# Queries and keys of a cosine attention, transposed by VectorE blocks and DMA through DRAM instead of by TensorE

## The chip, the cores and the metric

The kernel runs on one core of a Trainium2 chip. The metric is device time in microseconds (us) for one execution. The kernel is one program for a model of four layers. TensorE multiplies, and can transpose by multiplying with an identity matrix. VectorE, ScalarE and GpSimd work element by element or reduce along a row. SyncE issues the DMAs that concern us. Each engine works through its own list of instructions in the order in which the build put them, and waits where an input is not there yet.

## The reference

Input `x` is 2048 tokens of 512 features. Layer 0 is a rotary attention and a gated MLP, layer 2 a latent attention, layer 3 a set of grouped experts. The change is in layer 1, whose attention is a cosine attention. The kernel handles it as 8 batches of 256 tokens with 16 heads of 32 features; everything is f32:

```python
qkv = (xin @ Wqkv.T + qkv_bias)                  # q, k, v: 16 heads x 32
sm = exp(minimum(scale_mul_log, log(100)))       # one number for each head
qn = q / maximum(norm(q), 1e-12) * sm            # norm over the 32 features of a head
kn = k / maximum(norm(k), 1e-12)
p  = softmax(einsum('bhqd,bhkd->bhqk', qn, kn) + attn_bias)
o  = einsum('bhqk,bhkd->bhqd', p, v)
x  = x + (o @ Wproj.T + bproj) * gamma1
```

A query and a key come out of the projection with tokens on the partitions and features along the row. The scores need them turned, with the 32 features of a head on the partitions. That turn is what is changed.

## The kernel before

**Tiles.** A token tile is 128 tokens by 512 features; a batch is two of them, `t` = 0 and 1 (`TB` = 2). `KC` = 4 is the number of blocks of 128 features. PSUM is used in two rings of four banks: "A" for scores, "C" for all else. The tags `qT` and `kT` have two buffers each, `qk` four.

**The attention loop** (`attend`, line L655 on) has one round for each batch and each group of four heads, so 32 rounds. A round does this, in the program's order:

- `scored` (L697): eight score products for the four heads of the group, into four "A" banks.
- `turned` (L783): transposes by TensorE of the last group's weights of heads 2 and 3, first half.
- `softmax`: on VectorE a first pass (L743) that adds the bias and finds each row's lowest, on ScalarE the exponential (L747), eight of each. Heads 0 and 1 of a group are "in blocks" in all batches but the last: their weights are turned by VectorE in blocks of 32x32 (L752), written to DRAM in four DMAs (`put`, L549), and fetched back with the blocks in place (L756). For that their keys are read in runs of 32 elements. The other two heads' weights are turned by TensorE and copied out of PSUM (L480, L483).
- `some(quantum)`: work out of a queue (below).
- second half of `turned`, then `weighted` (L808: weights times v) and `divided` (L830, a context copy on VectorE that also divides), with `some` between.

**The queue** holds Python generators: the projection of the next batch (`project1`) and the outcome of the one before (`finish`: eight products with `w1o`, L631, then `gated`: a bias add on VectorE, L1454, and two multiplies/adds on GpSimd, L1455 and L1456). A generator yields after a bit of work and says what it took in us; `some` goes on until its credit is used. The credit of a batch is `work` = (22.1, 6.8), so many us for the projection and for the outcome, divided over the rounds. This sets only where in the program the work is written. A scheduler in the build then sets the order on every engine by priorities and its own costs.

**The projection** (`project1`, L1458 to L1535) does q and then k for t = 0 and for t = 1, then v for both. Each is four products of 128x512 (L631, through `part` and `product_steps`). For q VectorE adds the bias (L1495) and ScalarE squares (L1496); for k ScalarE squares (L1498) and copies (L1499). VectorE sums the squares for each head (L1501). GpSimd then takes a maximum with 1e-24 (L1503), the power -1/2 (L1504), for q a multiply with `sm` (L1506), and scales the tile (L1508). In the end `turned` (an inner function of the projection with the same name as that of the loop) turns each of the four tiles: four TensorE transposes into a "C" bank (L1479) and one copy into `qT` or `kT` (L480 on VectorE, L483 on ScalarE). The last eight transposes of a batch stand just ahead of the next batch's first scores.

**The start of the stage.** The projection of batch 0 is given to the MLP of layer 0 (`layer1_begin`), which works it off beside its last products (L1073).

Of the kernel before, what the change touches and what calls it, by code (L numbers as in the profile page):

```python
# [87 lines left out]
)  # L88
ROUND = 1.5 * 2.0**23
PI_BELOW = 3.1415925  # L90


def in_blocks(m):
# [86 lines left out]
class Program:  # L180
# [50 lines left out]
    def setup(self):  # L231
        nc, d = self.nc, self.d
        self.const = self.pool("const")
        self.xp = self.pool("xp")
        self.wqkvp = self.pool("wqkvp")
        self.wop = self.pool("wop")
        self.wbigp = self.pool("wbigp")
        self.work = self.pool("work")
        self.psum = self.pool("psum", psum=True)

        def c(shape, tag, **kw):
            return self.t(shape, tag, pool=self.const, **kw)

        self.condT = c([P, KC, 32], "condT")
        nc.gpsimd.memset(self.condT, 0.0)
        nc.sync.dma_start(
            self.condT[:, :, :B], d["condT"].rearrange("(k p) b -> p k b", p=P)
        )
        self.x = [self.t([P, D], f"x{i}", pool=self.xp) for i in range(NT)]
        self.tw = self.columns("tw1T", 1)  # L250
        for i in range(TB):
            self.load_x(i)
        self.vec = c([P, N_VEC], "vec")
        nc.sync.dma_start(self.vec, d["vec"])
        self.pos = c([P, NT], "pos", dtype=I32)
        nc.sync.dma_start(self.pos, d["posT"])
        self.inv_freq = c([P, 32], "inv_freq")
        nc.sync.dma_start(self.inv_freq, d["inv_freq"].to_broadcast([P, 32]))

        self.ident = c([P, P], "ident")  # L260
        make_identity(nc, self.ident)
        self.neg_half = c([P, 32], "neg_half")
        nc.gpsimd.memset(self.neg_half, -0.5)
        self.inv = [c([P, 32], f"inv{i}") for i in range(2)]
        for t in self.inv:
            nc.gpsimd.memset(t, 0.0)
        self.spread = [
            self.tc.dram_tile([32, P], F32, name=f"spread{i}") for i in range(4)
        ]
        self.n_spread = 0  # L270
        self.turns = [self.tc.dram_tile([P, KC * S], F32, name=f"turn{i}") for i in range(3)]
        self.n_turn = 0
        self.flips = [self.tc.dram_tile([P, 8 * P], F32, name=f"flip{i}") for i in range(4)]
        self.n_flip = 0
        self.half_pi = c([P, 1], "half_pi")
        nc.gpsimd.memset(self.half_pi, math.pi / 2)

        self.mod0 = c([P, 8, B], "mod0")
        self.mod1 = c([P, 16, B], "mod1")
        self.mod2 = c([P, 8, B], "mod2")  # L280
        self.mod3 = c([P, 8, B], "mod3")
        self.scondT = c([P, KC, 32], "scondT")
        nc.scalar.activation(self.scondT, self.condT, AF.Silu)
# [371 lines left out]
    def attend(self, name, n_groups, hd, project, value, finish, work, key_tiles=(2, 2), biased=None,  # L655
# [29 lines left out]
        def scored(b, g):  # L685
            lhs_rhs = [got[b][0](g, j) for j in range(4)]
            s = [self.bank("A") for _ in range(4)]
            rows = P // hd
            for j0 in range(0, 4, rows):
                for q in range(TB):  # L690
                    for j in range(j0, j0 + rows):
                        lhsT, rhs = lhs_rhs[j]
                        keys = rhs(wide[q])
                        if j < self.in_blocks(name, b):

                            keys = keys.rearrange("p (k c i) -> p c k i", c=4, i=32)
                        mm = nc.tensor.matmul(  # L697
                            s[j][:, at[q] : at[q] + wide[q]], lhsT(q), keys,
                            start=True, stop=True,
                        )  # L700

                        if name == "attention2" and j == q == 0:
                            self.tc.keep_in_program_order(mm)
            return s
# [562 lines left out]
    def project0(self, b, got):  # L1267
        nc, w, cos, sin = self.nc, self.w0, self.cos, self.sin
        hT = yield from self.h("attention0", b, quick=True)
        yield None  # L1270
        qT = self.t([P, KC, S], "qT")
        kT, v = self.keys_values(b, ((S,), (TB, 64)))
        turn = []
        for t in range(TB):
            i = TB * b + t
            cs, sn = cos[:, i, :], [s[:, i, :] for s in sin]
            tok = slice(t * P, (t + 1) * P)
            q = self.bank("C")
            yield from self.product_steps(q, lambda k: hT[:, k, tok], lambda k: w[:, k, 0:512])
            qr, qb = self.rope(self.bank("qk"), q, cs, sn, 8, 32)  # L1280
            nc.gpsimd.tensor_tensor(qr, qr, qb, ALU.add)
            kv = self.bank("C")
            yield from self.product_steps(
                kv[:, 0:128], lambda k: hT[:, k, tok], lambda k: w[:, k, 512:640]
            )

            kr = self.t([P, P], "kr", 2)
            ka, kb = self.rope(kr[:, 0:64], kv[:, 0:64], cs, sn, 1, 32)
            nc.vector.tensor_copy(v[:, t, :], kv[:, 64:128])
            nc.gpsimd.tensor_tensor(kr[:, 64:128], ka, kb, ALU.add)  # L1290
            nc.gpsimd.tensor_tensor(ka, ka, kb, ALU.add)
            turn.append((t, qr, kr))
        for t, qr, kr in turn:
            yield None
            self.queries_turned(t, qT, kT, qr, kr, 0.125)
            yield 0.53
        if b == 0:
            self.angles(cos, sin, slice(TB, 2 * TB))

        def scores(g, j):  # L1300
            c, i = divmod(4 * g + j, 2)
            rows = slice(64 * i, 64 * i + 64)
            return (
                lambda q: qT[rows, c, q * P : (q + 1) * P],
                lambda n: kT[rows, 0:n],
            )

        got[b] = (scores, v)
# [47 lines left out]
    def layer0_mlp(self):  # L1356
# [54 lines left out]
        def finish(hh, b, ys):  # L1411
# [6 lines left out]
        self.mlp(  # L1418
            ups, downs, down_sums, lambda i: self.layer0_up(4 + i, 1), load_next, act,
            lambda b: self.h("mlp0", b), finish,  # L1420
            (self.layer1_begin(), 22.1),
        )


# [33 lines left out]
    def project1(self, b, got):  # L1458
# [6 lines left out]
        yield None  # L1465

        def part(t, i):
            m = self.bank("C")
            yield from self.product_steps(
                m,  # L1470
                lambda k: hT[:, k, t * P : (t + 1) * P],
                lambda k: w[:, k, i * D : (i + 1) * D],
            )
            return m

        def turned(t, y, yT, at):
            m = self.bank("C")
            for c in range(KC):
                nc.tensor.transpose(  # L1479
                    m[:, c * P : (c + 1) * P], y[:, c * P : (c + 1) * P], self.ident  # L1480
                )
            self.copy(
                t + at, yT[:, :, t * P : (t + 1) * P], m.rearrange("p (c q) -> p c q", c=KC)
            )

        ready = []
        for t in range(TB):
            ss = self.t([P, 32], "ss", 2)
            both = []
            for i in range(2):  # L1490
                m = yield from part(t, i)
                y = self.bank("qk")
# [11 lines left out]
                nc.gpsimd.tensor_tensor(r, r, self.neg_half[:, 0:16], ALU.pow)  # L1504
                if i == 0:
                    nc.gpsimd.tensor_tensor(r, r, self.sm, ALU.mult)  # L1506
                by = r.unsqueeze(2).to_broadcast([P, 16, 32])
                nc.gpsimd.tensor_tensor(heads(y), heads(y), by, ALU.mult)  # L1508
                both.append(y)
            ready.append(both)  # L1510
        qT = self.t([P, KC, S], "qT")
        kT = self.t([P, KC, S], "kT")
        v = self.t([P, TB, D], "v")
        for t in range(TB):
            vp = yield from part(t, 2)
            nc.scalar.copy(v[:, t, :], vp)
            if t == 0:
                turned(0, ready[0][0], qT, 0)
                yield 0.43
                turned(0, ready[0][1], kT, 1)  # L1520
                yield 0.43
        yield None
        turned(1, ready[1][0], qT, 0)
        yield 0.43
        turned(1, ready[1][1], kT, 1)
        yield 0.43

        def scores(g, j):
            rows = slice(32 * j, 32 * j + 32)
            return (  # L1530
                lambda q: qT[rows, g, q * P : (q + 1) * P],
                lambda n: kT[rows, g, 0:n],
            )

        got[b] = (scores, v)  # L1535
# [1 line left out]
    def layer1_attention(self):  # L1537
# [29 lines left out]
        def value(v, g, j, k):  # L1567
            return v[:, k, (4 * g + j) * 32 : (4 * g + j + 1) * 32]

        self.attend(  # L1570
            "attention1", 4, 32, self.project1, value, finish, (22.1, 6.8),
            biased=(self.bias, self.bias_blocks),
            extra={
                4: (self.sums_of_ups(0, 2), 0.0), 5: (self.sums_of_ups(2, 4), 0.0),
# [91 lines left out]
    def project2(self, b, got):  # L1666
# [29 lines left out]
        def scores(g, j):  # L1696
            rows = slice(32 * j, 32 * j + 32)
            return (
                lambda q: qT[rows, g, q * P : (q + 1) * P],
                lambda n: kT[rows, 0:n],  # L1700
            )

        got[b] = (scores, v)
# [194 lines left out]
```

## Time and profile before

| | us |
|---|---|
| median of 3 runs (lowest, highest) | 2083.54 (2082.57, 2085.18) |
| the profiled execution | 2081.64 |
| its span | 2079.8 |
| mean granted TensorE clock in it | 0.989 of full speed |
| the cosine attention in it, from its first score to about the first work of its MLP | 908 to 1257 |
| busy in the whole span: TensorE, VectorE, ScalarE, GpSimd | 2009.4, 1346.3, 747.8, 315.3 |
| busy in 908 to 1257 (349 us): TensorE, VectorE, ScalarE, GpSimd | 343.0, 237.3, 207.0, 166.5 |

A line of a timeline or chain gives the start and the length in us, then engine, tile and source line. "SPq" is the queue of SyncE, on which the DMAs are issued. A name such as "PE C L1479 x8" is eight TensorE instructions of line 1479 that write a "C" bank. A matmul's own duration overlaps with its neighbours, so that a run of eight is shorter than eight times one. The first scores of the batches 0 to 7 start at 907.9, 956.1, 1000.9, 1044.6, 1088.2, 1131.8, 1175.4 and 1216.4 us.

### The profile page before, as it was taken

The numbers are of one execution on the slowest core, as the hardware profiler recorded it, in microseconds if no ns is written. First come the engines' busy times: TensorE is split into PE (matmuls) and PEld (weight loads), VectorE is DVE, ScalarE is ACT, GpSimd is POOL, SyncE is SP. The second block draws the span as 40 slices with busy tenths as digits, with TensorE's granted clock in tenths as the row PEclk, the third lists the DMA queues.
The fourth block names the chain that finished last, engine by engine and source line by source line (L and its number), as shares of the span: only waits on it lengthen the run. The fifth ranks groups of instructions, "written<-read, shape, count | busy, mean of one in ns | idle before, by whom it ended". The sixth has DMA issues, their size and how long they took to land.

```text
span 2079.8 us, 36181 instructions
## 1 busy us (share of the span) xinstructions
PE 2009.4 (97%) x12794; PEld 1469.7 (71%) x12794; DVE 1346.3 (65%) x4398; ACT 747.8 (36%) x2332; POOL 315.3 (15%) x348
## 2 busy tenths in 40 slices
PE   7899999999999999999999999999999989989998
PEld 4555579999999999954444448999999844445443
DVE  6767766656675555756676666766666788766333
ACT  4333331111111111136665653222222256566543
POOL 1111200000000000054545521000000031101120
PEclk9999999999999999999999999999999999999999
DMA  8543361112130000335455543334211245653001
GB/s 305 166 115 92 104 215 48 65 41 64 62 110 26 17 31 16 97 97 129 131 147 139 146 121 109 94 97 122 88 60 40 66 125 133 165 139 87 8 36 41
DMA packets 221523, 202.60 MB, mean 97 GB/s; under 512 B 83296, under 2 KB 184736, under 8 KB 221344
## 3 DMA queue, kind: packets, MB, share of 16 engines
q1 hardware_dynamic: 221344, 200.30, 33.1%
q8 instruction: 102, 1.67, 0.3%
q14 instruction: 77, 0.63, 0.1%
HBM read 132.31 MB, written 67.93 MB: 96 GB/s over the span
## 4 chain that ended last, share of the span: by engine, by line
PE 79%; DVE 7%; ACT 6%; DMA 3%; POOL 2%; issue 2%; SPq 1%; ACTq 0%; DVEq 0%; POOLq 0%
PE C L1024 29%; PE C L631 19%; PE A L1073 18%; PE A L697 4%; PE C L808 3%; ACT p L747 3%; ACT wbig L747 2%; PE C L783 2%; PE A L1766 1%; PE C L1785 1%; DVE st L449 1%; DVE n L650 1%; POOL ss L1504 1%; ACT p L483 1%; DMA turn<-hT 1%
## 5 line engine op out<-in xcount | busy, mean ns | idle before, releaser
L1024 PE MATMUL C<-hT,wbig 128*128 128x128 f32 x3072 | 416.4, 275 | 0.0
L1024 PEld LDWEIGHTS C<-hT,wbig 128*128 128x128 f32 x3072 | 388.8, 192 | 9.0 <-issue 2.4
L631 PE MATMUL C<-wqkv,hT 128*128 128x512 f32 (+1 forms) x768 | 313.4, 549 | 2.1 <-DVE p L480 0.8
L1073 PE MATMUL A<-wbig,p 128*128 128x256 f32 x1024 | 242.2, 379 | 0.0
L631 PEld LDWEIGHTS C<-wqkv,hT 128*128 128x128 f32 x768 | 132.1, 192 | 122.8 <-issue 107.0
L1073 PEld LDWEIGHTS A<-wbig,p 128*128 128x128 f32 x1024 | 189.7, 190 | 23.1
L1054 DVE TENSOR_TENSOR p<-p,C 128x256 f32<-128x256 f32 x192 | 78.9, 418 | 163.2 <-PE C L1024 161.4
L1044 ACT COPY p<-C 128x128 f32<-128x128 f32 x192 | 51.2, 267 | 370.4 <-PE C L1024 361.9
L1024 PE MATMUL C<-ctxT,wbig 128*128 128x128 f32 x1152 | 160.0, 275 | 0.0
L1024 PE MATMUL C<-qk,wbig 128*128 128x128 f32 x1152 | 160.0, 275 | 0.0
L747 ACT ACTIVATE p<-p,low 128x256 f32<-128x256 f32 x256 | 126.8, 497 | 70.0 <-DVE low L743 57.1
L457 POOL TENSOR_SCALAR r<-mv 128x2 f32<-128x2 f32 (+1 forms) x28 | 7.1, 253 | 946.7 <-DVE mv L450 946.7
L1024 PEld LDWEIGHTS C<-qk,wbig 128*128 128x128 f32 x1152 | 144.1, 192 | 0.0
L1024 PEld LDWEIGHTS C<-ctxT,wbig 128*128 128x128 f32 x1152 | 144.1, 192 | 0.0
L747 ACT ACTIVATE wbig<-wbig,low 128x128 f32<-128x128 f32 (+1 forms) x256 | 113.1, 443 | 77.1 <-DVE low L743 77.1
L1398 ACT ACTIVATE p<-C 128x128 f32<-128x128 f32 x64 | 17.8, 278 | 294.9 <-DVE p L1054 294.9
L1045 DVE TENSOR_TENSOR p<-p,C 128x128 f32<-128x128 f32 x192 | 54.6, 284 | 97.7 <-ACT p L1044 97.2
L631 PE MATMUL C<-wo,ctxT 128*128 128x512 f32 x224 | 103.1, 600 | 1.4 <-DVE ctxT L830 1.4
L1504 POOL TENSOR_TENSOR ss<-ss,neg_half 128x16 f32<-128x16 f32 x32 | 93.6, 2925 | 2.7
L747 ACT ACTIVATE p<-A,low 128x256 f32<-128x256 f32 x128 | 59.3, 485 | 87.8 <-DVE low L727 75.8
L697 PE MATMUL A<-kT,qT 32*128 32x256 f32 (+2 forms) x896 | 86.3, 399 | 0.7 <-DVE kT L480 0.4
L743 DVE CUSTOM_DVE_ANT_0 wbig<-A,row 128x128 f32<-128x128 f32 (+1 forms) x256 | 74.0, 351 | 13.5 <-PE A L697 13.4
(244 smaller groups left out, 3431.6 us busy)
## 6 DMA issues: line engine op xcount, KB each, us to landing
flip<-p SPq DMA_DIRECT2D x160, 128.0 KB
p<-flip SPq DMA_DIRECT2D x40, 512.0 KB
turn<-hT SPq DMA_DIRECT2D x120, 128.0 KB
flip<-wbig SPq DMA_DIRECT2D x112, 96.0 KB
wbig<-flip SPq DMA_DIRECT2D x28, 384.0 KB
hT<-turn SPq DMA_DIRECT2D x16, 512.0 KB
kept<-hT SPq DMA_DIRECT2D x16, 512.0 KB
hT<-kept SPq DMA_DIRECT2D x16, 512.0 KB
```

Source lines behind the costliest of these rows:

```text
L631: self.nc.tensor.matmul(out, lhsT(k), rhs(k), start=(k == 0), stop=(k == n - 1))
L697: mm = nc.tensor.matmul(s[j][:, at[q] : at[q] + wide[q]], lhsT(q), keys, start=True, stop=True,)
L743: nc.vector.tensor_tensor_reduce(out, src, by, -1.0, BIG, ALU.add, ALU.min, low[:, q : q + 1])
L747: nc.scalar.activation(out, src, AF.Exp, bias=low[:, q : q + 1], scale=sign, accum_out=tot[:, j, q : q + 1],)
L783: nc.tensor.transpose(m[:, n * P : (n + 1) * P], p[:, at[q] + k * P : at[q] + (k + 1) * P], self.ident,)
L808: mm = nc.tensor.matmul(o[i * hd : (i + 1) * hd, c * S + q0 * P : (c + 1) * S], value(got[b][1], g, j, k), weights(j, mine), start=(k == 0 ...
L1024: nc.tensor.matmul(m[:, c : c + P], w[:, k * P : (k + 1) * P], b[:, k], start=(first and k == 0), stop=(k == steps - 1), skip_group_check= ...
L1044: nc.scalar.copy(g[:, 0, :], m[:, 0:P])
L1045: nc.vector.tensor_tensor(g[:, 0, :], g[:, 0, :], m[:, P : 2 * P], ALU.add)
L1054: nc.vector.tensor_tensor(g[:, 1:3, :], g[:, 0, :].unsqueeze(1).to_broadcast([P, 2, P]), m[:, 2 * P : 4 * P].rearrange("p (i t) -> p i t", ...
L1073: nc.tensor.matmul(acc[at][:, half * S : (half + 1) * S], left, right, start=(p == 0 and half == 0), stop=(p == 3), skip_group_check=True,)
L1504: nc.gpsimd.tensor_tensor(r, r, self.neg_half[:, 0:16], ALU.pow)
```

## The change

GpSimd's scaling (L1508 of before) no longer works in place. It writes the scaled q and k of a token tile into one staging tile of 128x1024 (`stages[t]`, in the buffers of the tags `qT` and `kT`), in an order made for the turn. For each t one VectorE instruction turns q and k together in blocks of 32x32, and four DMAs (`put`) write the tile to a DRAM tile `pair`. When v's first tile has been copied, two DMAs for each t bring them back, with the blocks moved to their places: the queries into a `qk` bank, from which ScalarE copies them to `qT`, and the keys straight into `kT`. `qT` and `kT` lie in the same buffers as the staging tiles. The TensorE transposes of q and k, their "C" banks and their four copies are gone.

The keys now lie in another order, so the scores take them in runs of 32 elements for all heads; `keys_of` does for the other two attentions what the loop did before. The projection's products are declared to the queue at 0.75 of their time for q and k and at 1.5 for v, and the credit for a projection is 20.5 in place of 22.1.

```diff
+def keys_of(keys, blocks):
+    return keys.rearrange("p (k c i) -> p c k i", c=4, i=32) if blocks else keys
...
+        self.pairs = [self.tc.dram_tile([P, 8 * P], F32, name=f"pair{i}") for i in range(4)]
...
-                        keys = rhs(wide[q])
-                        if j < self.in_blocks(name, b):
-                            keys = keys.rearrange("p (k c i) -> p c k i", c=4, i=32)
+                        keys = rhs(wide[q], j < self.in_blocks(name, b))
...
-            (self.layer1_begin(), 22.1),
+            (self.layer1_begin(), 20.5),
...
         def part(t, i):
             m = self.bank("C")
-            yield from self.product_steps(
+            for us in self.product_steps(
                 m,
                 lambda k: hT[:, k, t * P : (t + 1) * P],
                 lambda k: w[:, k, i * D : (i + 1) * D],
-            )
+            ):
+                yield us * (1.5 if i == 2 else 0.75)
             return m
 
-        def turned(t, y, yT, at):
-            m = self.bank("C")
-            for c in range(KC):
-                nc.tensor.transpose(
-                    m[:, c * P : (c + 1) * P], y[:, c * P : (c + 1) * P], self.ident
-                )
-            self.copy(
-                t + at, yT[:, :, t * P : (t + 1) * P], m.rearrange("p (c q) -> p c q", c=KC)
-            )
+        stages = [self.t([P, KC * S], tag) for tag in ("qT", "kT")]
+        keeps = [self.pairs[(self.n_pair + t) % 4] for t in range(TB)]
+        self.n_pair += TB
         for t in range(TB):
+            put = stages[t].rearrange("p (c w k i) -> p w k c i", c=4, w=2, k=KC)
...
-                by = r.unsqueeze(2).to_broadcast([P, 16, 32])
-                nc.gpsimd.tensor_tensor(heads(y), heads(y), by, ALU.mult)
-                both.append(y)
-            ready.append(both)
-        qT = self.t([P, KC, S], "qT")
-        kT = self.t([P, KC, S], "kT")
+                by = r.rearrange("p (k c) -> p k c", c=4).unsqueeze(3)
+                nc.gpsimd.tensor_tensor(
+                    put[:, i], y.rearrange("p (k c i) -> p k c i", k=KC, c=4),
+                    by.to_broadcast([P, KC, 4, 32]), ALU.mult,
+                )
+            nc.vector.transpose(stages[t], stages[t])
+            self.put(keeps[t], stages[t])
+        qT, kT = stages[0].rearrange("p (k t) -> p k t", k=KC), stages[1]
         v = self.t([P, TB, D], "v")
         for t in range(TB):
             vp = yield from part(t, 2)
             nc.scalar.copy(v[:, t, :], vp)
             if t == 0:
-                turned(0, ready[0][0], qT, 0)
-                yield 0.43
-                turned(0, ready[0][1], kT, 1)
-                yield 0.43
-        yield None
-        turned(1, ready[1][0], qT, 0)
-        yield 0.43
-        turned(1, ready[1][1], kT, 1)
-        yield 0.43
+                for u in range(TB):
+                    kept = keeps[u].rearrange("p (a w x) -> p w a x", a=4, w=2)
+                    came = self.bank("qk")
+                    nc.sync.dma_start(came.rearrange("p (a x) -> p a x", a=4), kept[:, 0])
+                    nc.sync.dma_start(
+                        kT.rearrange("p (t a x) -> p t a x", t=TB, a=4)[:, u], kept[:, 1]
+                    )
+                    nc.scalar.copy(
+                        qT[:, :, u * P : (u + 1) * P].rearrange("p k (a j) -> p k a j", a=4),
+                        came.rearrange("p (a k j) -> p k a j", a=4, k=KC),
+                    )
+        kv = kT.rearrange("p (t a k j) -> p k t a j", t=TB, a=4, k=KC)
...
-                lambda n: kT[rows, g, 0:n],
+                lambda n, blocks: kv[rows, g].rearrange(
+                    "p t a j -> p a t j" if blocks else "p t a j -> p (t a) j"
+                ),
...
-            "attention1", 4, 32, self.project1, value, finish, (22.1, 6.8),
+            "attention1", 4, 32, self.project1, value, finish, (20.5, 6.8),
```

More of the change, by code (lines that the diff above doesn't have):

```diff
@@ L272, in setup @@
         self.n_turn = 0
+        self.pairs = [self.tc.dram_tile([P, 8 * P], F32, name=f"pair{i}") for i in range(4)]
+        self.n_pair = 0
         self.flips = [self.tc.dram_tile([P, 8 * P], F32, name=f"flip{i}") for i in range(4)]
@@ L1304, in scores @@
                 lambda q: qT[rows, c, q * P : (q + 1) * P],
-                lambda n: kT[rows, 0:n],
+                lambda n, blocks: keys_of(kT[rows, 0:n], blocks),
             )
@@ L1472, in part @@
                 lambda k: w[:, k, i * D : (i + 1) * D],
-            )
-            return m
-        def turned(t, y, yT, at):
-            m = self.bank("C")
-            for c in range(KC):
-                nc.tensor.transpose(
-                    m[:, c * P : (c + 1) * P], y[:, c * P : (c + 1) * P], self.ident
-                )
-            self.copy(
-                t + at, yT[:, :, t * P : (t + 1) * P], m.rearrange("p (c q) -> p c q", c=KC)
-            )
-        ready = []
+            ):
+                yield us * (1.5 if i == 2 else 0.75)
+            return m
+        stages = [self.t([P, KC * S], tag) for tag in ("qT", "kT")]
+        keeps = [self.pairs[(self.n_pair + t) % 4] for t in range(TB)]
+        self.n_pair += TB
         for t in range(TB):
+            put = stages[t].rearrange("p (c w k i) -> p w k c i", c=4, w=2, k=KC)
             ss = self.t([P, 32], "ss", 2)
-            both = []
             for i in range(2):
@@ L1699, in scores @@
                 lambda q: qT[rows, g, q * P : (q + 1) * P],
-                lambda n: kT[rows, 0:n],
+                lambda n, blocks: keys_of(kT[rows, 0:n], blocks),
             )
```

## The prediction

> **What bounds the kernel now.** I read the page first: TensorE is busy 97% of the span, so only what delays TensorE, or takes work from it, moves the time. Then windows over three whole batches of the cosine attention, from the first score of one batch to that of the next (columns: window, length, then busy time of TensorE, its weight loads, VectorE, ScalarE, GpSimd, then granted clock, DMA share, GB/s):
>
> ```profile
> 1044.56:1088.18 43.62, 43.50 (x241) 21.29 (x240) 29.78 (x100) 26.29 (x85) 23.27 (x20) 1.00 0.53 141
> 1088.18:1131.80 43.62, 43.51 (x241) 21.29 (x240) 29.80 (x100) 26.28 (x85) 23.27 (x20) 1.00 0.54 141
> ```
>
> TensorE idles 0.12 us in 43.62; the others have 14 to 20 us to spare. The chain of waits in the second window ends with the transposes that the change removes:
>
> ```profile
> 1128.90 1.05 PE C L808 x10
> 1129.96 1.02 PE C L1479 x8
> 1130.98 0.89 PE C L783 x8
> 1131.87 1.08 PE A L697 x16
> ```
>
> Eight L1479 take 1.02 us, so 16 a batch are 2.0 at most, 0.109 each in an unbroken run, thus 1.75 to 2.0. Eight batches: 14 to 16 us. That is all the change can save, as batches stand on TensorE without a gap.
>
> Next the timeline of GpSimd, because what is turned must first have been scaled there:
>
> ```profile
> 1071.25 0.25 POOL L1503 TENSOR_SCALAR ss<-ss 128x16 f32<-128x16 f32 x1
> 1071.59 2.92 POOL L1504 TENSOR_TENSOR ss<-ss,neg_half 128x16 f32<-128x16 f32 x1
> 1074.58 0.22 POOL L1506 TENSOR_TENSOR ss<-ss,sm 128x16 f32<-128x16 f32 x1
> 1074.88 1.05 POOL L1508 TENSOR_TENSOR qk<-qk,ss 128x512 f32<-128x512 f32 x1
> ```
>
> From a finished reduce (L1501) to a scaled q is 4.7 us (1071.25 to 1075.93), to a scaled k, which has no L1506, 4.4, of which the power L1504 is 2.92. Two gating multiplies (L1455, L1456) for a token tile of the previous batch's outcome add 1.27 each, 2.54. All go through one queue in order.
>
> **What goes from TensorE, and what comes.** Per batch 16 transposes and four copies out of PSUM go (two on VectorE, 0.69 and 0.65; two on ScalarE, 0.57). In come two block transposes on VectorE, priced by L534 with the same shape (128x1024, mean 1242 ns): VectorE +2.48 - 1.34 = +1.15 us, with 13.8 spare. ScalarE swaps two copies for two: 0. SyncE issues 8 puts and 4 fetches more; these rows
>
> ```profile
> 1117.67 1.76 SPq L549 DMA_DIRECT2D flip<-p  x4
> ...
> 1121.36 0.34 SPq L756 DMA_DIRECT2D p<-flip  x1
> ```
>
> of SyncE's timeline gives 0.44 us an issue, +5.3 a batch, and 1.9 us (1119.43 to 1121.36) until a fetch behind a put could go. GpSimd writes the same elements elsewhere: 0, since L1508's 1.05 already covers runs of 32. The scores now read keys in 32-element runs; two of four heads do that already, and their L697 takes the same 374 ns median as the others': 0. As work all this fits. The pacing (projection products at 0.75 for q and k, 1.5 for v, and 20.5 for 22.1) has no work of its own; it only moves where products stand, and the built order of the changed kernel contains that.
>
> A rule speaks against the change, and weighs differently here: the Trainium skill, "VectorE: DVE Perf Modes", sections "The three transpose paths" and "Rules for kernel authors", sends a 128x128 transpose to TensorE where PSUM can take it, with 390 ns there and 311 on VectorE for bf16. The rows here have 109 to 128 ns on TensorE and 1242/8 = 155 on VectorE in f32; by the page's 390 the removed work would be an estimated 50 us and the forecast some 35 us lower, and the rows decide.
>
> **Where it waits.** I laid the changed kernel's order on each engine beside the old one. Neither VectorE nor any other engine leaves its order. In a steady batch VectorE has: bias add of the outcome (L1454 of before), reduce of k tile 0, transpose of pair 0, context copy, bias add of q tile 1, its reduce, eight first softmax passes (L743) of group 2, its block transpose, reduce of k tile 1, transpose of pair 1, context copy, eight passes of group 3. Each pair transpose waits for GpSimd's scale of k, and everything named behind it waits too. Before, that wait was TensorE's, at a point where GpSimd had long been done; here GpSimd has just been given the work. GpSimd's order is q0, gating, k0, q1, k1.
>
> A walk of one batch, in us after its first score, by durations of the rows:
> - scores of groups 0 and 1 back to back: group 1 needs group 0's passes (8 x 0.345): 3.7; weighted sums 4.7; outcome products 8.15 and, with transposes and half of q1 between, 12.5.
> - L1454 0.67: 13.2. GpSimd gating 2.54: 15.8; k0 4.4: 20.2. Pair 0's transpose 1.24: 21.45. Context copy 0.42 and q1's bias add 0.67: 22.5. Before, VectorE would have done these two at about 14.
> - Square 0.63 and reduce 0.69: 23.9; GpSimd q1 4.7: 28.6. Group 2's passes 2.8: 26.7, exponentials 28.9; k1's square and reduce: 30.2; GpSimd k1: 34.6.
> - Pair 1's transpose: 35.9; context copy 36.3; group 3 from first pass to last exponential and copy 4.9 (1056.78 to 1061.68 in the trace): 41.2.
> - Copy out of PSUM and eight turns: 43.1. Then q0 and k0 of the next batch, which the order puts before its scores, 8 x 0.86 = 6.9: 50.0.
>
> Against 43.62 that is +6.4 with the saved 1.75 already in it. TensorE waits 43.62 - 1.75 = 41.9 of work against 50.0, some 8 us a batch, at group 2's scores and turns and at group 3's. Six batches: +38. The last round but one has no outcome products; its pair 0 stands ahead of group 0's passes: they start some 9 late, and some 5 of that is covered: +4.
>
> **The start of the stage.** The chain of waits there, rows of before:
>
> ```profile
> 890.95 2.94 POOL ss L1504
> 893.88 0.07 issue
> 893.95 1.05 POOL qk L1508
> ...
> 902.96 1.32 POOL qk L1508
> 904.28 0.04 issue
> 904.32 0.66 PE C L1479 x4
> 904.98 3.02 PE A L1073 x14
> 908.00 3.28 PE A L697 x17
> ```
>
> GpSimd runs its four chains without a gap from 886, as q tile 1's bias add was done at 889.3. Now that add stands behind pair 0's transpose: 895.0 + 1.24 + 0.67 = 896.9; square, reduce and handovers 1.6: 898.5; q1 903.2; k1 907.6; transpose 908.9; four issues 910.8; landing 912.7 (the 1.9). Fetches: the slowest 512 KB one in the trace took 4.19 us, these carry 256; I take 3.8 with issues, between 2 and 5: 916.5. ScalarE's copy 0.57: first score 917.1 in place of 907.9, +9.2 (7 to 11).
>
> Sum: 38 + 4 + 9.2 = +51. The profiled run is 2081.6 (span 2079.8, 1.8 around it): 2132.6. The median of the three is 1.9 higher, so 2134.5.
>
> **Rivals.**
> (1) Faster: GpSimd is done before VectorE asks. Then TensorE alone bounds; -14 to -16, and with the start's +9.2 about -6: 2077.5; with the start covered too, 2068.5. For it: GpSimd is only 53% busy. Against: it decides only if k's reduce stands 4.4 us (7 behind gating) ahead of the transpose, and the order has them adjacent. 0.13.
> (2) Only one wait a batch reaches TensorE, as queued turns and v products fill the other: half of 8 less 1.75, +2.3 x 6 + 7 at the start, +21: 2104; with less still, +1.4 x 6 + 7 = 2099, and down to the old time. For it: a hand walk tends to stack waits. 0.16.
> (3) More than the walk: the clock, or the queue of SyncE. The trace has a TensorE idle of 4.26 us around 64 to 68 and behind it the second row here; 1.6 us idle left no drop:
>
> ```profile
> 64.00:68.00 4.00, 0.00 (x0) 0.00 (x1) 1.54 (x4) 0.00 (x0) 0.00 (x0) 0.78 0.34 106
> 68.00:72.00 4.00, 4.00 (x42) 3.02 (x44) 3.11 (x11) 2.76 (x7) 0.00 (x0) 0.50 0.59 194
> 1206.00:1216.00 10.00, 8.36 (x61) 4.46 (x59) 7.57 (x25) 7.25 (x23) 0.00 (x0) 1.00 0.43 120
> ```
>
> About 5 us at half clock loses 2.5. The waits above come in pieces of 2.6 to 4 us: 0 to 2.5 a batch, 0 to 15 in all; I take 0 for the likeliest, since every piece is under 4.26, though nearer to it than to 1.6 at times. Likewise a put waiting in SyncE's queue for pair 1 (37.7) holds group 2's fetch behind it; I have it hidden by 4 us, and landing later it adds up to 3 a batch. Both ways 2150. 0.13.
> (4) The change doing nothing, or keys read slowly: the built order has no L1479 left, and the 374 ns speak against. Counted in (2).
>
> **How the numbers follow.** The forecast has 0.58, own range 2120 to 2147 (start 7 to 11, walk 5.5 to 8 a batch). The range reaches to (3)'s upper price and to (2)'s lower: 2092 to 2160; (1) and the lowest end of (2) are left out. 0.2%, 4.2 us, is about what a measurement of this kernel can tell from no change. Faster: (1), 0.13; within: the lowest of (2), 0.04; slower: 0.83.
>
> **What would show it.** Right: VectorE's waits on "POOL L1510" twice a batch of 3 to 6 us; from first score to first score about 50 us with TensorE idle 8; first score at about 917. Wrong: windows of 41.9 us with TensorE busy throughout (rival 1), one such wait (2), granted clock under 1.00 in steady batches (3).

## The result, and the profile after

The changed kernel takes 2185.85 us (median of four runs, 2182.76 to 2191.91) against 2083.76 before: 1.049 times as long, 95% interval 1.0475 to 1.0505. That is 102 us more, where 51 were forecast, and 26 us beyond the upper end of the stated range (2160). Its profiled span is 2183.4 us at a mean granted clock of 0.965 (0.989 before).

Two whole batches in the windows view, with the columns of the prediction's first fence:

```profile
1148.91:1206.80 57.89, 51.20 (x225) 24.23 (x225) 30.68 (x99) 26.78 (x84) 23.34 (x21) 0.85 0.57 151
1206.80:1264.79 57.99, 51.29 (x225) 23.99 (x224) 30.68 (x99) 26.79 (x84) 23.34 (x21) 0.85 0.52 140
```

A batch takes 57.9 us instead of 43.6. VectorE, ScalarE and GpSimd are within 1 us as busy as before; TensorE now idles 6.7 us, is busy 7.7 us longer with less work, and its clock is 0.85. Both have to be explained. The waits of VectorE over the same two batches (us in total, times, longest) name what was forecast:

```profile
DVE qT L1514 <- POOL qT L1510: 13.0, 2, 6.5
DVE kT L1514 <- POOL kT L1510: 9.0, 2, 4.5
```

Each pair transpose stands 4.5 to 6.5 us in VectorE's queue until GpSimd has scaled k. The chain of waits goes through just these instructions:

```profile
1166.04 0.70 DVE n L1459
1166.81 1.28 POOL n L1460
1168.15 1.27 POOL x L1461
1169.73 2.94 POOL ss L1506
1172.74 1.06 POOL qT L1510
```

The outcome's bias add, its two gating multiplies, then the chain of k0: 7.0 us from VectorE's add to the scaled k, and behind it the transpose. In the chain of a whole batch of before (1088 to 1132 us, its end is in the prediction), no instruction of GpSimd stood at all.

### The profile page after: what moved, and what is told of

It reads as the page before. It is cut to its first block, busy times and chain, and to the rows that moved or that the text cites. A ratio compares the mean times of both kernels' runs of the same rounds, so it can differ in the third digit from the quotient of the medians.

```text
span 2183.4 us, 36037 instructions
## 1 busy us (share of the span) xinstructions
PE 2038.7 (93%) x12666; PEld 1480.4 (68%) x12666; DVE 1355.6 (62%) x4398; ACT 751.0 (34%) x2332; POOL 315.6 (14%) x348
## 4 chain that ended last, share of the span: by engine, by line
PE 69%; DVE 9%; DMA 6%; ACT 6%; POOL 6%; issue 3%; SPq 2%; ACTq 0%; DVEq 0%; POOLq 0%
PE C L1029 27%; PE A L1078 17%; PE C L638 13%; ACT p L752 3%; POOL ss L1506 3%; PE A L702 3%; PE C L813 2%; PE C L788 2%; ACT wbig L752 1%; PE A L1776 1%; DMA turn<-hT 1%; DMA p<-flip 1%; DVE p L748 1%; PE C L1795 1%; DVE st L456 1%
## 5 line engine op out<-in xcount | busy, mean ns | idle before, releaser
L638 PE MATMUL C<-wqkv,hT 128*128 128x512 f32 (+1 forms) x768 | 325.0, 565 | 3.2 <-DVE p L487 0.8
L638 PEld LDWEIGHTS C<-wqkv,hT 128*128 128x128 f32 x768 | 136.7, 198 | 132.4 <-issue 115.8
L464 POOL TENSOR_SCALAR r<-mv 128x2 f32<-128x2 f32 (+1 forms) x28 | 7.2, 256 | 949.3 <-DVE mv L457 949.3
L702 PE MATMUL A<-kT,qT 32*128 32x256 f32 (+2 forms) x896 | 96.3, 421 | 37.0 <-DMA kT<-pair 20.3
L702 PEld LDWEIGHTS A<-kT,qT 32*128 32x128 f32 (+1 forms) x896 | 60.4, 203 | 82.1 <-issue 61.3
L813 PE MATMUL C<-p,v 128*32 128x256 f32 (+1 forms) x640 | 72.7, 439 | 44.2 <-ACT p L490 28.6
L638 PE MATMUL C<-wo,ctxT 128*128 128x512 f32 x224 | 105.2, 611 | 1.9 <-DVE ctxT L835 1.9
```

The lines of the kernel that those rows point to most:

```text
L638: self.nc.tensor.matmul(out, lhsT(k), rhs(k), start=(k == 0), stop=(k == n - 1))
L702: mm = nc.tensor.matmul(s[j][:, at[q] : at[q] + wide[q]], lhsT(q), keys, start=True, stop=True,)
L813: mm = nc.tensor.matmul(o[i * hd : (i + 1) * hd, c * S + q0 * P : (c + 1) * S], value(got[b][1], g, j, k), weights(j, mine), start=(k == 0 ...
```

## The experiments

Differences below are from the median of the kernel before in the same comparison; the interval behind a ratio is the 95% one. Line numbers are each kernel's own. "The trip" is the way of a pair tile through DRAM: put, landing, fetch, landing. In the profile `kT<-pair` is the fetch of turned keys, and `p<-flip` that of a group's turned weights, which was there before.

### Taking the power away, in the changed kernel and in the one before

```diff
-                nc.gpsimd.tensor_tensor(r, r, self.neg_half[:, 0:16], ALU.pow)
```

> The changed kernel without the power -1/2 on GpSimd (L1506), so queries and keys are scaled by their sums of squares instead; everything else stays, and every engine keeps the same order of instructions. Theory A (VectorE waits in its own queue for GpSimd's chain, and all behind it waits too): the chain of k falls from 4.4 to 1.4 us, the walk of one batch from 50 to about 44, VectorE's two waits for L1510 together from 22 us in two batches to under 6, and the clock comes back with the idle time: 2095 us (2085 to 2115). Theory B (the trip through DRAM and SyncE's queue bound it): most of the loss stays, above 2160. In between: both.

Measured: 2122.4 us, ratio 1.019 [1.0155, 1.0225], +39 in place of +102. The order on every engine is that of the changed kernel, so 63 us follow from 2.9 us less in each of four chains a batch. The two batches from 1061.49 us take 48.7 and 49.0 us (the first six lie between 47.5 and 55.8), and the granted clock is back at 0.981. VectorE still waits for GpSimd in these two:

```profile
DVE qT L1513 <- POOL qT L1509: 7.0, 2, 3.5
DVE kT L1513 <- POOL kT L1509: 3.0, 2, 1.5
```

Less came back than theory A gave, more than theory B allowed.

> The kernel before without the same power. Control: there GpSimd's chain lies beside TensorE except at the start of the stage. Theory A and B alike: the steady batches stay at 43.6 us, the first score comes up to 9 us earlier: 2078 us (2073 to 2084).

Measured: 2083.25, ratio 0.9998 [0.9989, 1.0008]. The same 2.9 us cost nothing before. The first score came only 1.7 us earlier (906.26); the other 7 of my guess were covered by other work of TensorE. A duration has no price of its own: it depends on who waits for it.

### The pacing alone, in the kernel before

> The kernel before with the new pacing alone (projection products declared at 0.75 for q and k and 1.5 for v, credit 20.5 for 22.1), transposes by TensorE as before. TensorE has the same work and no new wait: within 4 us of before under either theory. Over 10 us slower would mean that the moved products, not the turn, cost time.

Measured: 2085.4, ratio 1.0011 [1.0002, 1.0021], +2. The moved products are not the cause.

### When the transposes stand, and whether there is a trip

Four kernels make a square: the changed one; one with its transposes held back behind the passes of group 3; and both of these without puts and fetches.

```diff
-            nc.vector.transpose(stages[t], stages[t])
-            self.put(keeps[t], stages[t])
...
             nc.scalar.copy(v[:, t, :], vp)
+            self.tc.keep_in_program_order(nc.vector.transpose(stages[t], stages[t]))
+            self.put(keeps[t], stages[t])
```

> The changed kernel with the two block transposes of a batch and their puts and fetches held back to after the v products and pinned there in VectorE's order (pair 0 and pair 1 both behind the passes of group 3). Theory A: VectorE's waits for GpSimd fall under 1 us a batch, softmax is no longer held, but the trip now starts at about 37 us of a batch and ends at about 47, so 4 to 5 us a batch remain: 2126 us (2100 to 2150). Theory B: later trips make it worse, 2185 or above.

> The changed kernel without the trip through DRAM: the eight puts and four fetches of a batch are left out, so the blocks are not moved to their places; ScalarE's copies and VectorE's transposes with their waits stay. The order on TensorE, VectorE and ScalarE moves somewhat with it. Waits that the trip holds up directly (kT<-pair 20 us, flips behind the puts 11) go and so does part of the clock: 2145 us (2130 to 2165) if the wait for GpSimd is the larger cause, under 2110 if the trip is.

> The changed kernel with its block transposes pinned behind the passes of group 3 as in the run with late transposes, and without the trip (eight puts and four fetches a batch left out); power, pacing, VectorE's transposes and ScalarE's copies stay. If wait and trip are the whole cause: 2083 us (2075 to 2089). If pacing, VectorE's work or the reading of keys in runs of 32 costs the 14 us that were left before: 2095 or more.

| | with the trip | without the trip |
|---|---|---|
| transposes where the build put them | +102 | +76 (2157.7, 1.0368 [1.0343, 1.0392]) |
| transposes held back | +96 (2179.3, 1.0458 [1.0435, 1.048]) | +6 (2089.8, 1.0028 [1.0019, 1.0038]) |

Either of the two is enough for most of the loss: the wait in VectorE's queue 76 us without any trip, a trip that is begun late 90 us (96 against 6) while VectorE waits for GpSimd only at the start of the stage (7.3 and 8.6 us). With both gone 6 us are left. That the two overlap in the changed kernel, because the trip of the next batch has time while TensorE waits for VectorE, is my reading of the square. The 90 us are the price of the late trip, not of the trip as the changed kernel has it: there, leaving it out is worth 26 us. Without puts and fetches the build also orders TensorE's work somewhat differently, so the columns differ in a little more than the trip. I expected 2126 of the late transposes, since I gave the trip 8 to 10 us. The chain of that kernel shows what it takes:

```profile
1132.34 1.14 DVE kT L1519
...
1136.02 4.58 DMA pair<-kT
1140.62 0.55 SPq L1525
1141.20 0.62 SPq L1524
1141.87 4.54 DMA kT<-pair
1146.55 2.09 PE A L702 x16
```

From the end of the transpose (1133.48) to the first score it is 13.1 us: four issues with two of the softmax between them, 4.58 from the last of them until the put has landed, two issues, 4.54 until the fetch has.

### Both taken away with the transposes where the build put them

> Both taken away: no power on GpSimd and no trip through DRAM. If these two are the whole cause, TensorE alone bounds the batches at 41.9 us and the saved transposes show: 2068 us (2062 to 2080). If something else is left (the pacing, VectorE's extra work, keys read in runs of 32), 2085 or above.

> No power and no trip (2098 us before), and TensorE's products q and k of tile 0 pinned behind the first scores of the batch, as they stand in the kernel before (from batch 1 on). If the order of TensorE is what was left: 2083 us (2075 to 2088). If the waits of VectorE that remain (28 us in all) are: 2093 to 2102.

Measured: 2097.8, 1.0069 [1.0046, 1.0092], and with the products pinned 2098.0, 1.0068 [1.0054, 1.0082]. That is 16 us above before, the second branch of the first expectation. TensorE's order round the first scores is not what was left. VectorE still waits 28 us for GpSimd in both, and that is the candidate, not tested by itself: where the held-back transposes do not wait, 6 us are left with the power in place. The pin on the whole change:

> The changed kernel whole, with the same pin. VectorE's wait for GpSimd stays, and the products no longer cover the trip (13 us). If the order was a large cause, 2150 to 2170; if it was the build's answer to the late trip and covered it, 2186 or more.

Measured: 2196.3, 1.0539 [1.0517, 1.056], some 10 to 12 us worse than unpinned. The build's order does cover a part of the trip: TensorE's waits for `kT<-pair` in the stage are 34.5 us here and 20.3 in the changed kernel.

### No turn at all, in the kernel before

```diff
         def turned(t, y, yT, at):
-            m = self.bank("C")
-            for c in range(KC):
-                nc.tensor.transpose(...)
             self.copy(
-                t + at, yT[:, :, t * P : (t + 1) * P], m.rearrange("p (c q) -> p c q", c=KC)
+                t + at, yT[:, :, t * P : (t + 1) * P], y.rearrange("p (c q) -> p c q", c=KC)
             )
```

> The kernel before without any turn of queries and keys: the 16 TensorE transposes of a batch are left out, the copies read the scaled tiles instead. The most that the change could have saved: 14 to 16 us, 2068 us (2066 to 2072).

Measured: 2150.1, 1.0327 [1.031, 1.0344], 68 us slower, with 16 transposes a batch gone and nothing in their place. Its waits of VectorE, over the whole stage, say why:

```profile
DVE kT L480 <- POOL qk L1503: 34.9, 8, 4.5
DVE qT L480 <- POOL qk L1503: 32.4, 7, 4.8
```

VectorE's copies now read what GpSimd has scaled, not what TensorE has transposed, and the build puts them early. It is the changed kernel's wait, without a block transpose and without a DMA.

> The kernel before without any turn (the transposes by TensorE are left out, the copies read the scaled tiles), as in the run that was 68 us slower, but with the four copies pinned at their place in the program, behind what VectorE and ScalarE were given before them. If those 68 us were VectorE's queue standing before GpSimd's scaling, they go, and the 14 to 16 us of the transposes show: 2068 us (2066 to 2076). If not, above 2120.

Measured: 2083.3, ratio 0.9998 [0.9986, 1.0009]. The 68 us are gone, but the 14 to 16 us do not show. One batch of it, and the first score of the next in TensorE's timeline:

```profile
1087.61:1130.94 43.33, 41.74 (x225) 19.58 (x225) 29.19 (x100) 26.25 (x84) 23.24 (x20) 1.00 0.54 142
```

```profile
1130.94 0.50 PE L697 MATMUL A<-kT,qT 32*128 32x256 f32 x4 [1.08 <-DVE kT L480]
```

TensorE works 1.76 us less and the batch is 0.29 us shorter; the batches beside it are the same within 0.01 us. The transposes had filled time in which the first scores' inputs, and half a microsecond of group 2's weights, were not there yet. In this kernel the copies are pinned, so a better place for them might show a part; it was not tried.

### Half of the change

Only token tile 0 of batches 1 to 7 goes through VectorE and DMA, its transpose pinned where GpSimd is done with it; tile 1 stays on TensorE.

> Half of the change: in batches 1 to 7 only token tile 0 is turned by VectorE and DMA, its block transpose pinned behind k's reduce of tile 1, when GpSimd has long scaled tile 0; tile 1, and batch 0, stay on TensorE. Old pacing, credit 21.2. If a transpose that does not wait for GpSimd and a trip begun by about 32 us of a batch are harmless, eight TensorE transposes a batch are saved: 7 x 0.9 to 1.0, 2076 us (2074 to 2080). If the trip (13 us from transpose to score in the run with late transposes) comes too late for scores at 43 us, or SyncE's queue holds flips, 2084 to 2110.

> The same with tile 0's transpose pinned one step earlier, behind q's reduce of tile 1. Same expectation, and up to 1 us a batch better than the other where the trip is late: 2076 us (2073 to 2080).

> The half change with tile 0's transpose behind q's reduce of tile 1 (2106 us before), and the same pin. If TensorE's order cost the 23 us: 2078 to 2088. If the trip or SyncE's queue did: 2098 or more, with TensorE waiting for kT<-pair at each first score.

> As half_pin, with the transpose some 1.5 us earlier and the fetch issued ahead of the put of group 3's flip. If the trip was late in half_pin, this one is better by what TensorE waited there: 2076 to 2083, the eight transposes a batch saved being worth at most 7. Otherwise the same as half_pin.

| | us | ratio |
|---|---|---|
| behind k's reduce of tile 1 | 2114.0 | 1.0148 [1.0129, 1.0167] |
| behind q's reduce | 2106.0 | 1.0116 [1.0098, 1.0134] |
| that, products behind the first scores | 2100.6 | 1.0082 [1.0067, 1.0096] |
| that, earlier still, fetched ahead of the next flip | 2122.2 | 1.0186 [1.0171, 1.0201] |

All are slower than before. The third came out as the second branch of its expectation said (2098 or more, with waits for `kT<-pair`); the other three missed. In the first two, TensorE's longest waits are for the weights' fetch `p<-flip` (12.3 and 14.5 us in the stage). In the third, its waits over three batches of 45.5 to 47.1 us are almost one line:

```profile
PE A L706 <- DMA kT<-pair: 11.6, 4, 3.3
```

Tile 0's transpose begins 29 to 30 us into a batch, and in the batch from 1051.60 its puts are issued by 33 us. But the fetch of the keys is issued only at 41.8 us, in SyncE's queue behind the put of group 3's weights, and comes about 3 us late. In the fourth, whose fetch stands ahead of that put, the trip is in time (1.0 us of that wait in the whole stage). TensorE's transposes of tile 1 wait for GpSimd instead (17.3 us in seven waits), and two waits for `p<-flip` take 8.6 us. Why GpSimd is later there was not followed up.

### Idle work for TensorE

> The changed kernel with idle work for TensorE where it waits longest in a batch: in the weighted sums of group 1, 24 matmuls of 32x256 (3.0 us by the 0.125 us of L813's) ahead of head 3, in group 2 six (0.75 us), into rows that the next matmul overwrites; 26 us of work in seven batches. It tells apart whether the clock that the changed kernel loses (TensorE's busy time is 29 us longer with 15 us less work, 44 us) lies on the path. If it does, the granted clock comes back to over 0.98 and the time falls to 2140 to 2165 us. If the slow clock only fills time in which TensorE would have waited anyway, 2180 to 2195.

> The changed kernel with idle work for TensorE in one wait only, that of group 1's weighted sums: 10 matmuls of 32x256 at the 0.23 us that the first filler run showed, 2.3 us in a wait of 3.28, in batches 0 to 6. If TensorE's clock drops for that wait, and if the slow clock lies on the path, steady batches go from 57.9 to about 53.7 us: 2165 us (2155 to 2175). If the wait alone decides, 2183 to 2190.

Measured: 2206.1, 1.0598 [1.0577, 1.062] at a clock of 0.978, and 2190.9, 1.0521 [1.0505, 1.0537] at 0.968. Both were mis-sized. In the trace a filler is two matmul records of about 0.2 us each, so 24 of them stand some 10 us on TensorE, not 3.0, and ten some 4 us in a wait of 3.28. The first raised TensorE's busy time by 65 us and tells little.

The second tells something about one stretch, the slow clock behind the wait in group 1's weighted sums. In its batch from 1152.18 to 1209.70 the clock stays at 1.00 from 1180 to 1195, where the changed kernel has 0.81 and 0.51. Group 3's scores start 38.3 us after the first score of the batch instead of 40.5. Yet the batch takes 57.5 us instead of 57.9, for then TensorE waits for group 2's weights:

```profile
1198.17 2.07 PE L821 MATMUL C<-p,v 128*32 128x256 f32 x16 [3.83 <-DMA p<-flip]
```

This fetch has landed 46.0 us into the batch in either kernel; the changed kernel waits 1.39 us for it. So the slow clock in that stretch has next to no price of its own, because a second path is as long.

None of the versions run beats the kernel before.

## Why the prediction was wrong in size

The direction, the mechanism and the place were right: VectorE waits for GpSimd twice a batch at the pair transposes, softmax stands behind, and rival 1 did not happen. Rival 2 did in part: in the chain of the batch of 57.9 us only the first of the two waits stands, and the second acts beside it (SyncE's queue, below). Its price, half a wait, did not come. Three terms of the sum were too small: the walk of one batch (38 us in all, measured 74.5), the start (9.2, measured 14.9) and the last round but one (4, measured 10.1). In the walk, the steps that failed are the scores of group 1, sized at 3.7 us, and the clock of TensorE, taken at nothing.

**The walk of one batch** gave 50.0 us. Measured from first score to first score: 56.0, 56.7, 59.7, 53.7, 57.9 and 58.0 for batches 0 to 5. Against the rows of before that is 74.5 us. Batches 0 to 2 were not walked through. In the batch of 57.9 the steps go apart in three places.

- Group 1's scores end 6.1 us after the first score, not 3.7. They take a bank only when a pass of group 0 has freed it, and the scores of the last bank come after the last pass.
- From there the outcome ends at 17.1 instead of 12.5: 2.4 of it is the late scores, 2.0 is a slow clock (weighted sums 1.86 us for 1.00, eight matmuls L638 4.78 for 3.63). GpSimd's part behind it is as forecast, 7.0.
- In group 1's weighted sums TensorE waits 3.28 us for a copy that stands behind the held-up exponentials, and runs slowly again behind it: 1.91 for 1.05, and 3.71 for 1.91.

```profile
1183.81 1.91 PE L813 MATMUL C<-p,v 128*32 128x256 f32 x10 [3.28 <-ACT p L490]
```

**The clock**, where I had written 0 to 2.5 us a batch and taken 0, has a price in the second place. The batch just before shows it: it has the same instructions, in the same order but for a few of VectorE near its end, and the same two waits of TensorE (0.94 us ahead of group 1's scores, 3.27 in its weighted sums). It takes 53.7 us, with a granted clock of 0.94 where the next has 0.85:

```profile
1095.24:1148.91 53.67, 46.59 (x225) 22.34 (x224) 30.52 (x99) 26.67 (x84) 23.32 (x21) 0.94 0.55 149
1097.33 3.10 PE L702 MATMUL A<-kT,qT 32*128 32x256 f32 x16 [0.94 <-DVE low L748]
...
1151.00 4.04 PE L702 MATMUL A<-kT,qT 32*128 32x256 f32 x16 [0.94 <-DVE low L748]
```

There the sixteen scores of group 1 take 3.10 us instead of 4.04 and the matmuls behind them run at their old pace, so the outcome ends at 14.1 us instead of 17.1. That is 3.0 of the 4.2 us between the two batches. In the third place the run with ten idle matmuls found next to no price; its own two batches, with the clock at full there, still differ by 3.8 us (53.7 and 57.5). So rival 3 had the right thing, but neither its 0 nor its 2.5 us a batch: two of the batches lose some 3 to 4 us by the clock, and for the first three it is not known.

Its lower end had no ground in the rows. The windows of the kernel before hold, some 40 us ahead of its rows, these two as well:

```profile
24.00:28.00 4.00, 1.97 (x10) 1.12 (x10) 2.62 (x13) 0.94 (x3) 3.08 (x6) 1.00 1.05 387
28.00:32.00 4.00, 3.47 (x17) 2.26 (x17) 3.21 (x13) 2.16 (x6) 0.94 (x2) 0.59 1.04 387
```

TensorE's longest idle time there is 1.24 us, with ten transposes between the pieces, and the clock fell to 0.59 and then 0.50. That every piece is under 4.26 was no bound.

**SyncE's queue**, the other part of rival 3, was not hidden by 4 us either. In the batch of 57.9 the puts of group 2's weights are issued by 1184.51, but their fetch goes at 1189.84, just behind the first put of pair 1 (1189.32), which waits for VectorE's transpose. At the 1.9 us of the prediction it could have gone some 3 us earlier. It makes TensorE wait 1.39 us, and it is the second path of the run with ten idle matmuls.

**The start** was +14.9 (first score at 922.83), not +9.2. GpSimd ended at 910.24 instead of 907.6, because its first power began 2.9 us later than before. That shift comes from ahead of the stage, where GpSimd's instruction before it (L464, L457 of before) already starts 2.9 us later; in the profiles of the other runs it starts anywhere from 2.6 us earlier to 3.9 later than before, so it need not be the change's. And the trip took 12.6 us from there, not 9.5:

```profile
909.18 1.06 POOL kT L1510
...
910.26 1.26 DVE kT L1514
```

```profile
922.83 2.09 PE L702 MATMUL A<-kT,qT 32*128 32x256 f32 x16 [15.01 <-DMA kT<-pair]
```

The put landed about as priced: the last issue ends at 913.29, and the fetch that waits for it goes at 915.30. The fetches were mis-sized. The last of the four, of keys, is issued at 916.54, behind the others and a load of weights, so that from 915.30 to the first score it is 7.5 us where the sum had 4.4. Its 3.8 us came from a single fetch, the only one that the chain of the stage shows (4.19).

**The last round but one** lost 10.1 us, not 4.

14.9 + 74.5 + 10.1 = 99.5 of the 102.

**The stated range** is a little wider than its terms: a start of 7 to 11 and a walk of 5.5 to 8 a batch give about 2127 to 2146, not 2120 to 2147.

**What the change could save** was wrong too, though it did not decide. "That is all the change can save, as batches stand on TensorE without a gap" took 43.50 busy of 43.62 as proof that every instruction taken away shortens the batch. With all turns gone and nothing in their place, 0.29 of 1.76 us a batch came back. Rival 1's 2068 to 2077 was not reached in any run, not even in the one with no turn, whose VectorE waits for scaled queries and keys at the start of the stage alone (2083.3).

The costs put at nothing held together to within the +6 of the run with neither wait nor trip: VectorE's extra work, ScalarE's copies, keys in runs of 32, and the pacing (+2 alone). That is net of what the missing transposes saved there.

## What to carry to other kernels

An operation moved to an engine with spare time costs what stands behind it in that engine's queue while it waits for its input: look where in the queue it lands, and how far its producer is at that moment. A bound engine that is 99.7% busy may still be waiting underneath; before an expected saving is believed, take the work away and put nothing in its place. A way through DRAM is two landings and their issues one after the other, and is paid in full if it begins later than its length before the need.

## What the runs showed of the hardware

TensorE's clock fell at shorter gaps than I had allowed for (windows of the changed kernel, the granted clock is the third figure from the end):

```profile
1150.00:1155.00 5.00, 4.06 (x24) 2.68 (x20) 4.33 (x19) 4.06 (x16) 2.28 (x3) 0.74 0.30 111
1155.00:1160.00 5.00, 5.00 (x22) 2.13 (x22) 3.14 (x17) 2.52 (x10) 0.00 (x0) 0.58 0.62 149
1180.00:1185.00 5.00, 1.72 (x15) 0.60 (x16) 2.51 (x6) 4.24 (x14) 3.33 (x5) 0.81 0.67 124
1185.00:1190.00 5.00, 5.00 (x14) 1.76 (x16) 1.55 (x2) 0.00 (x0) 2.93 (x2) 0.51 0.22 60
```

The last is behind the idle time of 3.28 us. The first two rows cover 0.94 us of idle time, then 4.04 us in which 16 scores, 1.1 us of work, came one by one as banks were freed, and what follows. The record calls that stretch busy; the clock did not take it so. In the batch before, the same 0.94 us and 16 scores over 3.10 us (1097.33 on) left the clock at 1.00, so neither length decides by itself. The Trainium skill, "TensorE: Matmul & The Clock Gate", section "What's actually happening", states a free-running activity window of about 3.4 us. The idle time of 3.28 us before the 0.51 row is just under that and a window can fall on nearly all of it; no run here tells how thinly spread matmuls count in it.

A put of four DMAs and a fetch through DRAM took 4.58 and 4.54 us to land in the chain with late transposes, with 256 KB in a fetch. The same put took 2.37 us in a chain of the changed kernel (1175.44 on).
